# Symmetric attention: blocks of 1024 queries that meet whole blocks of keys, changed to halves of 512 that meet in a circle (72 units a pair of heads for 80)

## The chip, the core and the metric

The kernel runs on one core of one Trainium2 chip. Its engines have queues of their own: PE (TensorE) multiplies matrices, ACT (ScalarE) does the exponentials, DVE (VectorE) transposes and adds, POOL (GpSimd) copies small pieces, SP (SyncE) issues most transfers. The metric is the device time of one execution in microseconds (us); before the change it is 7413.25 us, the median of three runs (7411.64 to 7416.1).

## The reference, cut to what matters

Two layers work on an image batch of 4 x 128 channels x 64 x 64, so 4096 tokens an image. The first layer is a group norm, 1x1 convolutions and a channel-wide attention, the second an attention over 16 heads of 8 numbers, a feed-forward part and a recurrence. The change lies in the attention of the second layer. Query, key and value are the same array there, so the score matrix is symmetric:

```python
qkv = _qz_ring(heads + rx_theta)
q = jnp.transpose(qkv, (0, 2, 1, 3))
scores = jnp.einsum('bhsd,bhtd->bhst', q, q) / np.sqrt(D)
attn = jax.nn.softmax(scores, axis=-1)
ctx = jnp.einsum('bhst,bhtd->bhsd', attn, q)
```

The array that comes in is 4 x 4096 x 128. The denominators need no maximum taken off first, since the scores are bounded.

## The kernel before, in words

The images are worked on one after the other: a convolution stage (`first_stage`), then the attention (`second_stage`, which calls `attention`), and the feed-forward part of an image runs beside the convolution stage of the next. The last image's feed-forward part stands alone (`third_stage`), and the recurrence ends the program.

**Units.** `attention` loops over 8 pairs of heads. For each it cuts the 4096 tokens into 4 blocks (NQB) of 1024 queries and 32 tiles of 128 keys. A unit is one tile of keys against one block of queries, for both heads of the pair: 4 score matmuls (L839: two heads h, two halves x of 512 queries), 2 exponentials of 128x1024 on ACT (L848), and, two units later, `weigh` (L717), which multiplies the exponentials by the values and adds up in one PSUM bank `acc` for the whole block.

**Symmetry.** A block b meets its own 8 tiles (own units) and only the tiles of the blocks `behind` it in a circle: the next two blocks for b = 0 and 1, the next one for b = 2 and 3. `order` interleaves them. What the other blocks of queries would have needed is taken from the same exponentials, transposed. For an off-diagonal unit ACT also writes the sums over the queries (`accum_out`, an extra accumulator-read instruction on ACT) into `denom`; DVE transposes the two tiles of exponentials (`run_flips`, L684) into `flipped`, two more instructions; and PE multiplies them by `mirror` weights in `mirror_step` (L697). Four units make a group; a group takes 16 mirror steps of 8 matmul instructions, and after the last DVE adds the result into `later` (L708, L710).

**The order by hand.** PE, ACT, DVE and POOL follow program order in this stage. In each turn (one unit) come: scores, exponentials, `weigh` of the unit two turns back, as many mirror steps as a credit allows (`rates` is what a unit adds to it; at most 4.0 is kept), the steps that are due in `ends`, and up to two units' transposes (none in the first unit of a block). A group's steps may begin two turns after its fourth transposition was issued, and a group's first transposition waits until the group two before it is used up (`flipped` holds two groups).

**The end of a block.** `finish` runs when a block's last unit has been weighed, in the second unit of the next block: DVE transposes `acc` (o, L745), POOL copies it to `own` (L753, 16 copies). `mirrored` adds what other blocks left in `later` and `denom`: POOL copies the sums into order (L738), DVE transposes `later` (turned, L765), POOL copies (other, L772) and adds (L774, L775). `result` divides on DVE (L779, L780). For blocks 1 to 3 `mirrored` comes at once and `result` 6 turns later; block 0's wait for the next pair's block 0.

**Buffers.** `exps` (6) and parts of the image `xs` hold exponentials of five units; `ps_pair` (3 buffers of two PSUM banks) holds scores; `ps_acc` 1; `keys` 6 blocks; `turned` 2, shared by turned and other.

Of the kernel before, what the change touches and what calls it, by code (L numbers as in the profile page):

```python
# [26 lines left out]
def kernel(  # L27
# [32 lines left out]
    P = 128  # L60
# [498 lines left out]
    def attention(n, q, xs, tail, upcoming):  # L559
# [8 lines left out]

        qb = blocks(q)
        fixed, _ = here["fixed"]  # L570

        behind = [[(b + 1 + i) % NQB for i in range(2 if b < NQB // 2 else 1)] for b in range(NQB)]
        met_by = [[b for b in range(NQB) if k in behind[b]] for k in range(NQB)]
# [18 lines left out]
        def prepare(pair):  # L592
# [51 lines left out]
            later = get("later", f"later{n}_{pair}")  # L644
            denom = get("denom", f"denom{n}_{pair}")
# [44 lines left out]
        def mirror_step(state, s):  # L690
# [4 lines left out]
            for h in range(2):  # L695
                for x in range(2):
                    nc.tensor.matmul(  # L697
                        state["acc"][ts(2 * h + x, 32), :],
# [6 lines left out]
            if s == 15:  # L705
                dst = state["later"][:, ts(state["batch"], P)]
                if state["slot"] == 0:
                    nc.vector.tensor_copy(dst, state["acc"])  # L708
                else:
                    nc.vector.tensor_tensor(dst, dst, state["acc"], ALU.add)  # L710

        def weigh(it):
            if it["first"]:
                it["in"]["acc"] = get("ps_acc", "acc{}_{}_{}".format(n, *it["block"]))
            for h in range(2):
                for x in range(2):
                    nc.tensor.matmul(  # L717
                        it["in"]["acc"][ts(2 * h + x, 32), :],
                        it["qa"][:, ds((2 * it["jt"] + h) * V, 32)],
# [5 lines left out]

        def mirrored_sums(pair, b, denom):

            total = denom[:, 0, ts(b, QT), :]
            for slot in range(1, len(met_by[b])):
                by_key = small.tile([P, QT, 2], F32, tag="by_key", name=f"by_key{n}_{pair}_{b}")  # L730
                nc.gpsimd.tensor_tensor(by_key, total, denom[:, slot, ts(b, QT), :], ALU.add)
                total = by_key
# [8 lines left out]
        def finish(pair, b, block, later, denom):  # L741
# [5 lines left out]
            tag = "own" if b else "own_0"  # L747
# [9 lines left out]
            def mirrored():  # L757
# [6 lines left out]
                turned = get("turned", f"turned{n}_{pair}_{b}")  # L764
                nc.vector.transpose(turned, later[:, ts(b, 2 * P)])  # L765
                tv = turned.rearrange("p (y k a d) -> p k y a d", y=2, k=4, a=4)
                other = get("turned", f"other{n}_{pair}_{b}")[:, 0 : QT * 2 * D]
                to = other.rearrange("p (y a h d) -> p h y a d", y=2, a=4, h=2)
                for x in range(2):
                    for h in range(2):  # L770
                        for k in range(4):
                            nc.gpsimd.tensor_copy(to[ts(k, 32), h], tv[ts(2 * h + x, 32), k])  # L772
# [14 lines left out]
            if b:  # L787
                ends.append((turn, mirrored))
                ends.append((turn + 6, result))
            else:  # L790
                first.extend([mirrored, result])

        def order(b):

            own = list(range(QT * b, QT * (b + 1)))
            rest = [jt for k in behind[b] for jt in range(QT * k, QT * (k + 1))]
            each = len(rest) // QT
            return [
                jt for k in range(QT) for jt in rest[each * k : each * (k + 1)] + own[k : k + 1]
            ]  # L800

# [13 lines left out]
        ends, first = [], []  # L815
# [3 lines left out]
        for pair in range(NPAIR):  # L819
            keys, queries, qa, later, denom = ready  # L820
            for b in range(NQB):
# [7 lines left out]
                for at, jt in enumerate(tiles):  # L829
                    assert not (tail and jt // QT == NQB - 1)  # L830
                    name = f"{n}_{pair}_{b}_{jt}"
                    cols = ts(jt % QT, P)
                    off = jt // QT != b
                    slot = met_by[jt // QT].index(b) if off else None
                    ss = [pair_psum(f"s{name}_{h}") for h in range(2)]
                    for h in range(2):
                        for x in range(2):
# [3 lines left out]
                                keys[jt // QT].bitcast(F32R)[r, cols],  # L841
# [4 lines left out]
                    es = exps(name, end_of_all and at >= 2)  # L846
                    for h in range(2):
                        nc.scalar.activation(  # L848
                            es[h],
                            ss[h].rearrange("p x c -> p (x c)"),  # L850
# [82 lines left out]
        for _, end in ends[:-2]:  # L933
            end()
# [213 lines left out]
    def first_stage(im, before):  # L1148
# [11 lines left out]
        with stage(f"conv{n}", **pools, **psum), tc.manual_schedule(engines=engines):  # L1160
# [4 lines left out]
            def meanwhile(steps=1):  # L1165

                calls[0] += 1
                if before and calls[0] in (10, 11):
                    before["left"].pop(0)()
# [324 lines left out]
```

## Time and profile before

| | |
|---|---|
| runs | 7416.1, 7413.25, 7411.64 us; median 7413.25 |
| profiled execution | 7414.47 us, its span 7412.7 us, mean granted TensorE clock 0.984 |
| busy share of the span | PE 96%, ACT 82%, DVE 73%, PEld 46%, POOL 37% |
| attention stretches (434.6 to 1712.2, 2245.1 to 3522, 4054.2 to 5332, 5866.8 to 7145) | 1277.6, 1276.9, 1277.8, 1278.2 us |
| convolution stretches between them | 532.9, 532.2, 534.8 us |
| start to the first attention, and after the last | 434.6 and 267 us |

All times in the profile are us from the span's start unless marked ns. A group line names the line of the kernel, the engine, the operation, what is written and read, how often, then the busy time, the mean length of one instruction in ns and the engine's idle time before it. Instructions of PE, ACT and DVE overlap their neighbours a little, so the distance from start to start is shorter than the length. A busy PE need not be a PE at its peak.

### The profile page before, as it was taken

The numbers are of one execution on the slowest core, as the hardware profiler recorded it, in microseconds if no ns is written. First come the engines' busy times: TensorE is split into PE (matmuls) and PEld (weight loads), VectorE is DVE, ScalarE is ACT, GpSimd is POOL, SyncE is SP. The second block draws the span as 40 slices with busy tenths as digits, with TensorE's granted clock in tenths as the row PEclk, the third lists the DMA queues.
The fourth block names the chain that finished last, engine by engine and source line by source line (L and its number), as shares of the span: only waits on it lengthen the run. The fifth ranks groups of instructions, "written<-read, shape, count | busy, mean of one in ns | idle before, by whom it ended". The sixth has DMA issues, their size and how long they took to land. (4 is left out here: it accounts for less than half of the span.)

```text
span 7412.7 us, 212494 instructions
## 1 busy us (share of the span) xinstructions
PE 7153.2 (96%) x88078; PEld 3385.8 (46%) x88078; DVE 5395.9 (73%) x7364; ACT 6107.7 (82%) x9557; POOL 2730.3 (37%) x9769
## 2 busy tenths in 40 slices
PE   8999999999999999999899999999999999999977
PEld 3444444444444444444444444444444444444446
DVE  5677777776777777777677777777767777777764
ACT  3479999995448999999445999999844599999976
POOL 1034444343223434344323343444422243444342
PEclk9999999999999999999999999999999999999989
DMA  0010000000111000000011100000001100000012
GB/s 27 32 38 24 25 21 21 19 9 25 35 39 43 26 20 20 23 22 18 18 36 45 35 21 19 24 24 18 18 26 35 48 26 23 23 23 24 11 58 103
DMA packets 81537, 211.99 MB, mean 29 GB/s; under 512 B 8800, under 2 KB 8832, under 8 KB 79792
## 3 DMA queue, kind: packets, MB, share of 16 engines
q1 hardware_dynamic: 77312, 186.68, 7.4%
q8 instruction: 693, 11.35, 0.7%
q10 hardware_dynamic: 2016, 10.49, 0.3%
q14 instruction: 284, 2.33, 0.1%
q0 software_dynamic: 1232, 1.14, 0.1%
HBM read 141.65 MB, written 56.62 MB: 27 GB/s over the span
## 5 line engine op out<-in xcount | busy, mean ns | idle before, releaser
L848 ACT ACTIVATE e<-s 128x1024 f32<-128x1024 f32 x3144 | 3102.2, 1042 | 24.2 <-PE s L839 12.5
L684 DVE STREAM_TRANSPOSE t<-e 128x1024 f32<-128x1024 f32 x1896 | 2210.3, 1212 | 296.8 <-ACT e L848 296.7
L697 PEld LDWEIGHTS misc<-t,mirror 128*32 128x32 f32 x49152 | 1449.2, 110 | 1482.2 <-issue 1453.2
L848 ACT ACTIVATE xs<-s 128x1024 f32<-128x1024 f32 x1976 | 1960.5, 1040 | 13.3 <-PE s L839 2.3
L697 PE MATMUL misc<-t,mirror 128*32 128x128 f32 x49152 | 1801.0, 273 | 0.0
L717 PE MATMUL acc<-e,q_aug 128*32 128x512 f32 x12576 | 1682.6, 607 | 0.0
L684 DVE STREAM_TRANSPOSE t<-xs 128x1024 f32<-128x1024 f32 x1176 | 1372.6, 1211 | 195.7 <-ACT xs L848 195.7
L753 POOL COPY own<-o 32x36 f32<-32x36 f32 x2048 | 429.0, 209 | 2612.5 <-DVE o L745 2532.6
L839 PE MATMUL s<-queries,keys 32*128 32x512 f32 x10240 | 1372.8, 495 | 16.9 <-ACT e L848 15.5
L717 PE MATMUL acc<-xs,q_aug 128*32 128x512 f32 x7904 | 1053.3, 605 | 0.0
L407 PE MATMUL acc<-p,asmT 128*128 128x512 f32 x2048 | 982.9, 612 | 0.0
L392 ACT ACTIVATE p<-s 128x1024 f32<-128x1024 f32 x512 | 497.2, 1022 | 557.3 <-PE s L384 548.2
L839 PEld LDWEIGHTS s<-queries,keys 32*128 32x128 f32 x10240 | 535.4, 181 | 607.9 <-issue 279.5
L400 DVE TENSOR_TENSOR total<-total,p 128x1024 f32<-128x1024 f32 x448 | 575.0, 1284 | 298.2 <-ACT p L392 274.8
L654 POOL COPY mirror<-q 32x128 f32<-32x128 f32 x2048 | 604.2, 295 | 107.4 <-PE misc L697 19.7
L407 PEld LDWEIGHTS acc<-p,asmT 128*128 128x128 f32 x2048 | 360.7, 191 | 516.5 <-issue 514.3
L384 PE MATMUL s<-e,e 64*128 64x512 f32 x2048 | 521.8, 628 | 4.6 <-DVE asmT L301 4.3
L772 POOL COPY other<-turned 32x64 f32<-32x64 f32 x2048 | 474.0, 231 | 87.4
L717 PEld LDWEIGHTS acc<-e,q_aug 128*32 128x32 f32 x12576 | 250.2, 108 | 387.5 <-issue 379.0
L848 ACT ACTIVATION_READ_ACCUMULATOR e<-s 128x1 f32 x1896 | 418.7, 221 | 0.0
L384 PEld LDWEIGHTS s<-e,e 64*128 64x128 f32 x2048 | 179.7, 190 | 276.8 <-issue 263.4
L717 PEld LDWEIGHTS acc<-xs,q_aug 128*32 128x32 f32 x7904 | 156.3, 108 | 242.0 <-issue 226.3
(243 smaller groups left out, 4679.8 us busy)
## 6 DMA issues: line engine op xcount, KB each, us to landing
keys<-parts_dram SPq DMA_DIRECT2D x256, 256.0 KB
queries<-parts_dram SPq DMA_DIRECT2D x1024, 32.0 KB
fx<-x_dram SPq DMA_DIRECT2D x64, 256.0 KB
x_dram<-x SPq DMA_DIRECT2D x56, 256.0 KB
xs<-in_x_dram SPq DMA_DIRECT2D x16, 512.0 KB
t_dram<-t2T SPq DMA_DIRECT2D x32, 256.0 KB
t2s<-t_dram SPq DMA_DIRECT2D x16, 512.0 KB
parts_dram<-high SPq DMA_DIRECT2D x28, 256.0 KB
```

The lines of the kernel that those rows point to most:

```text
L384: nc.tensor.matmul(s[:, j, :], e2[rows, ts(2 * jp + j, P)], e1[rows, ts(ic, IC)], start=True, stop=True,)
L392: nc.scalar.activation(p, s, AF.Exp)
L400: nc.vector.tensor_tensor(state[ic], state[ic], p, ALU.add)
L407: nc.tensor.matmul(state["acc", ic], asmT[:, ts(2 * jp + j, P)], p[:, j, :], start=jp == 0 and j == 0, stop=jp == NP - 1 and j == 1,)
L654: nc.gpsimd.tensor_copy(wv[ts(a, 32), s, :, :, ts(a, D)], own[ts(s, 32)])
L684: nc.vector.transpose(group["e"][h][:, k, :], es[h])
L697: nc.tensor.matmul(state["acc"][ts(2 * h + x, 32), :], state["w"][:, QT * (s // 4) + TG * x + s % 4, h, :], state["e"][h][:, :, ds(IC * x ...
L717: nc.tensor.matmul(it["in"]["acc"][ts(2 * h + x, 32), :], it["qa"][:, ds((2 * it["jt"] + h) * V, 32)], it["e"][h][:, ts(x, IC)], start=it[ ...
L753: nc.gpsimd.tensor_copy(own[ts(s, 32), ts(x, 4), h, :], ov[ts(2 * h + x, 32), s, :, 0:V])
L772: nc.gpsimd.tensor_copy(to[ts(k, 32), h], tv[ts(2 * h + x, 32), k])
L839: nc.tensor.matmul(ss[h][:, x, :], keys[jt // QT].bitcast(F32R)[r, cols], queries[b].bitcast(F32R)[r, :], start=True, stop=True,)
L848: nc.scalar.activation(es[h], ss[h].rearrange("p x c -> p (x c)"), AF.Exp, scale=1.0 / math.sqrt(D), accum_out=denom[:, slot, jt, h : h + ...
```

## The change

The unit stays 128 keys against 1024 queries, but the two halves of the queries may now meet different tiles of keys. The eight half blocks of 512 stand in a circle; each meets itself and the next four halves (in blocks 0 and 1) or three (in blocks 2 and 3). An own unit pairs tile k of a block's first half with tile k of its second (4 units for 8). Most off-diagonal units use one tile for both halves, as before; four in each block are split, half x of the queries against tile `unit[x]`. A split unit has four exponentials of 512 columns, each with its own accumulator read, and its group is added into `later` in two halves. Blocks have 20, 20, 16 and 16 units for 24, 24, 16 and 16; of them 16, 16, 12 and 12 are off-diagonal, for 16, 16, 8 and 8.

With it: `denom` is laid out anew; `later` is cleared by POOL, and every group is added to it; `mirrored` and `result` of block 2 run in block 3, those of blocks 3, 0 and 1 in the next pair's block 0 (in its ninth, fourteenth and nineteenth unit, each `result` five turns later); after the last pair these three run at the end with scratch rooms of their own, and their results move into the next stage; the feed-forward part starts with block 2; the rates of the credit change; `turned` and `other` get a buffer each.

```diff
-        behind = [[(b + 1 + i) % NQB for i in range(2 if b < NQB // 2 else 1)] for b in range(NQB)]
-        met_by = [[b for b in range(NQB) if k in behind[b]] for k in range(NQB)]
+        met_by = [sorted((k - i) % NQB for i in range(3)) for k in range(NQB)]
...
+            nc.gpsimd.memset(later, 0.0)
...
-                        state["acc"][ts(2 * h + x, 32), :],
+                        state["acc"][ts(2 * x + h, 32), :],
...
-                dst = state["later"][:, ts(state["batch"], P)]
-                if state["slot"] == 0:
-                    nc.vector.tensor_copy(dst, state["acc"])
-                else:
-                    nc.vector.tensor_tensor(dst, dst, state["acc"], ALU.add)
+                whole = state["batch"][0] == state["batch"][1]
+                for x in range(1 if whole else 2):
+                    rows = slice(0, P) if whole else ts(x, P // 2)
+                    dst = state["later"][rows, ts(state["batch"][x], P)]
+                    nc.vector.tensor_tensor(dst, dst, state["acc"][rows, :], ALU.add)
...
-                        it["qa"][:, ds((2 * it["jt"] + h) * V, 32)],
+                        it["qa"][:, ds((2 * it["tiles"][x] + h) * V, 32)],
...
+        def third_sum(b):
+            return 2 * NT + (b - NQB // 2) * TG
...
+            total = small.tile([P, QT, 2], F32, tag="by_key", name=f"by_key{n}_{pair}_{b}")
+            nc.gpsimd.tensor_tensor(
+                total, denom[:, ts(b, QT), :], denom[:, ds(NT + b * QT, QT), :], ALU.add
+            )
+            if b >= NQB // 2:
+                odd = total[:, TG:QT, :]
+                nc.gpsimd.tensor_tensor(odd, odd, denom[:, ds(third_sum(b), TG), :], ALU.add)
...
-            if b:
-                ends.append((turn, mirrored))
-                ends.append((turn + 6, result))
-            else:
-                first.extend([mirrored, result])
+            if b == 2:
+                ends.append((turn + 8, mirrored))
+                ends.append((turn + 12, result))
+            elif b > 2:
+                late[0:0] = [mirrored, result]
+            else:
+                late.extend([mirrored, result])
...
-            own = list(range(QT * b, QT * (b + 1)))
-            rest = [jt for k in behind[b] for jt in range(QT * k, QT * (k + 1))]
-            each = len(rest) // QT
+            own = [(QT * b + k, QT * b + TG + k) for k in range(TG)]
+            halves = [(v, v) for v in range(2 * b + 2, 2 * b + (5 if b < NQB // 2 else 4))]
+            halves.insert(2, (2 * b + 1, 2 * b + (5 if b < NQB // 2 else 4)))
+            rest = [
+                tuple(v % (2 * NQB) * TG + k for v in vs) for vs in halves for k in range(TG)
+            ]
+            each = len(rest) // TG
+            return [u for k in range(TG) for u in rest[each * k : each * (k + 1)] + own[k : k + 1]]
...
+                    split = off and unit[0] != unit[1]
                     for h in range(2):
...
+                        for x in range(2 if split else 1):
+                            nc.scalar.activation(
+                                es[h][:, ts(x, IC)] if split else es[h],
+                                ss[h][:, x, :] if split else ss[h].rearrange("p x c -> p (x c)"),
+                                AF.Exp,
+                                scale=1.0 / math.sqrt(D),
+                                accum_out=denom[:, sums_at(b, unit[x]), h : h + 1] if off else None,
+                            )
-                    rates = (2.9, 2.2) if len(behind[b]) == 2 else (2.2, 1.9)
+                    rates = (3.3, 3.0) if b < NQB // 2 else (3.15, 3.0)
...
-                    if b == 0 and at == 10 and pair:
-                        ends.append((turn, first.pop(0)))
-                        ends.append((turn + 6, first.pop(0)))
+                    if b == 0 and pair and at in (7, 12, 17):
+                        ends.append((turn, late.pop(0)))
+                        ends.append((turn + 5, late.pop(0)))
...
-        first[0]()
-        ends.append((0, first[1]))
-        for _, end in ends[:-2]:
+        for _, end in ends:
             end()
-        return [end for _, end in ends[-2:]]
+        rooms = (None, half_tile(f"room0_{n}"), get("later", f"room1_{n}"))
+        for mirrored, room in zip(late[0::2], rooms):
+            mirrored(room)
+        return late[1::2]
...
-        order = [(i + NTG // NQB) % NTG for i in range(NTG)]
+        order = [(i + 2 * NTG // NQB) % NTG for i in range(NTG)]
...
-                if before and calls[0] in (10, 11):
+                if before and calls[0] in (10, 14, 18):
...
-            denom=((P, 2, NT, 2), 2),
-            later=((P, NT * 32), 2),
-            half=(HALF, 1),
-            turned=((P, 2 * P), 2),
+            denom=((P, 2 * NT + NQB // 2 * TG, 2), 2),
+            later=((P, NT * 32), 2),
+            half=(HALF, 1),
+            turned=((P, 2 * P), 1),
+            other=((P, QT * 2 * D), 1),
```

## The prediction, made before the changed kernel was run

> **What bounds the kernel now.** I read the 40 slices first: each image has an attention stretch where PE and ACT both stand at 9, and a convolution stretch where ACT stands at 4. I then cut one pair of heads (image 1, pair 6, whose units begin at 3044.2) into its four blocks of queries.
>
> ```profile
> core 0: us, PE busy (x) PEld busy (x) DVE busy (x) ACT busy (x) POOL busy (x), PEclk, DMA share, GB/s
> 3044.20:3092.60 48.40, 48.40 (x788) 23.19 (x784) 40.02 (x44) 48.16 (x82) 23.39 (x103) 1.00 0.07 26
> 3092.60:3141.00 48.40, 48.40 (x807) 23.38 (x800) 38.40 (x38) 48.14 (x81) 12.59 (x48) 1.00 0.03 8
> 3141.00:3171.50 30.50, 30.50 (x460) 13.82 (x456) 20.50 (x23) 30.49 (x49) 15.52 (x67) 1.00 0.09 28
> 3171.50:3202.60 31.10, 31.10 (x466) 14.04 (x458) 20.89 (x23) 30.98 (x50) 15.73 (x68) 1.00 0.10 32
> sum 158.40, PE 158.40 PEld 74.43 DVE 119.81 ACT 157.77 POOL 67.24; mean PE 39.60 PEld 18.61 DVE 29.95 ACT 39.44 POOL 16.81
> ```
>
> A pair takes 158.4 us, PE and ACT both look full, and shares cannot say which sets the pace. Starts can, so I read the timeline of PE inside the first block:
>
> ```profile
> 3050.34 0.51 PE L839 MATMUL s<-queries,keys 32*128 32x512 f32 x4
> 3050.78 1.07 PE L717 MATMUL acc<-e,q_aug 128*32 128x512 f32 x8
> 3051.66 0.84 PE L697 MATMUL misc<-t,mirror 128*32 128x128 f32 x24
> 3052.43 0.50 PE L839 MATMUL s<-queries,keys 32*128 32x512 f32 x4
> ...
> 3054.51 0.51 PE L839 MATMUL s<-queries,keys 32*128 32x512 f32 x4
> 3054.95 1.06 PE L717 MATMUL acc<-xs,q_aug 128*32 128x512 f32 x8
> 3055.84 0.62 PE L697 MATMUL misc<-t,mirror 128*32 128x128 f32 x16
> 3056.39 0.51 PE L839 MATMUL s<-queries,keys 32*128 32x512 f32 x4
> ```
>
> One unit runs from one L839 to the next. With 24 L697 matmuls (3 mirror steps of 8) it takes 2.09 us, with 16 (2 steps) 1.88; elsewhere in the block 2 steps give 1.87 and 4 give 2.31. So a unit costs PE 1.434 us plus 0.218 per step. Blocks 0 and 1 have 24 units each and 64 steps (four groups of 16): 24 x 1.434 + 64 x 0.218 = 48.4, exactly the window: PE sets the pace there. Blocks 2 and 3 give 16 x 1.434 + 32 x 0.218 = 29.9, but take 30.5 and 31.1. ACT says why:
>
> ```profile
> 3145.52 1.02 ACT L848 ACTIVATE e<-s 128x1024 f32<-128x1024 f32 x1
> 3146.44 0.19 ACT L848 ACTIVATION_READ_ACCUMULATOR e<-s 128x1 f32 x1
> 3146.53 1.02 ACT L848 ACTIVATE e<-s 128x1024 f32<-128x1024 f32 x1
> 3147.43 0.20 ACT L848 ACTIVATION_READ_ACCUMULATOR e<-s 128x1 f32 x1
> 3147.53 2.85 ACT L848 ACTIVATE e<-s 128x1024 f32<-128x1024 f32 x3
> ```
>
> Start to start an exponential with its accumulator read takes 1.00 us, one without 0.90 (about 0.10 being the read). An off-diagonal unit costs ACT 2.00, an own unit 1.80; 8 + 8 of them make 30.4, so ACT holds blocks 2 and 3, by 0.5 to 1.2 us each. The DVE lines are the third resource:
>
> ```profile
> L684 DVE STREAM_TRANSPOSE t<-e 128x1024 f32<-128x1024 f32 x1896 | 2210.3, 1212 | 296.8 <-ACT e L848 296.7
> L1004 ACT ACTIVATE hT<-ph,fb_sb 128x512 f32<-128x512 f32 x128 | 80.8, 683 | 62.8 <-PE ph L1001 62.6
> L294 ACT ACTIVATE ya<-pca,b_sb 128x1024 f32<-128x1024 f32 x16 | 17.9, 1119 | 64.1 <-PE pca L343 63.8
> DVE later L708 <- PE misc L697: 7.0, 6, 1.7
> DVE o L745 <- PE acc L717: 6.6, 4, 2.9
> DVE later L710 <- PE misc L697: 4.9, 3, 1.7
> DVE inv L779 <- POOL own L775: 4.5, 3, 1.7
> ```
>
> The last four are waits within that one pair. DVE is idle 158.4 - 119.8 = 38.6 us there.
>
> **The change, step by step.** Units per pair fall from 80 (24, 24, 16, 16) to 72 (20, 20, 16, 16). Own units fall from 32 to 16; off-diagonal ones rise from 48 to 56, groups from 12 to 14. Of the 56, 16 are split: two key tiles, so four 512-column exponentials with four reads.
>
> PE: blocks 0 and 1 become 20 x 1.434 + 64 x 0.218 = 42.6, blocks 2 and 3 16 x 1.434 + 48 x 0.218 = 33.4; the pair 152.1. The new credit rates feed this: 16 x 3.3 + 4 x 3.0 = 64.8 steps for 64, 12 x 3.15 + 4 x 3.0 = 49.8 for 48. Matmul shapes stay. Against 158.4: -6.3, of which 4.5 is PE work (156.6 to 152.1) and 1.8 is what ACT held back.
>
> ACT: no 512-column exponential is in the trace. Relu at 512 takes 683 ns (L1004) and at 1024 1119 (L294): 512 columns less save 436. So it starts 0.90 - 0.44 = 0.46 to 0.47 apart, and a split unit costs 4 x (0.47 + 0.10) = 2.26. The bound above: it keeps Relu's fixed part, 2 x 683 - 1119 = 247 ns against 1025 - 2 x 436 = 153 for the exponential, so 0.09 more each, 2.65 a unit; below, two halves cost one whole plus two reads, 2.2. I take 2.26, as the slope is per column and the fixed part is the exponential's own. Blocks 0 and 1: 4 x 1.80 + 12 x 2.00 + 4 x 2.26 = 40.2 under PE's 42.6; blocks 2 and 3: 7.2 + 16 + 9.0 = 32.2 under 33.4. ACT drops below PE everywhere.
>
> The Trainium skill speaks against the split ("ScalarE: Activation LUTs", What ACT_TABLE_LOAD costs): every ACTIVATE has a fixed part, about 186 ns with immediate scale and bias, plus 0.833 ns a column, and neighbours overlap by about 93. By it 512 columns would be 0.52 apart and a split unit an estimated 2.5; ACT would need 33.1 of 33.4 in blocks 2 and 3, and the sum would lose up to 1 us a pair. At 1024 columns the same rule gives 0.95 where this trace has 0.90.
>
> The split units come three or four in a row. ACT falls behind by 2.26 - 2.09 = 0.17 a unit, 0.5 to 0.7 after the row, and the three buffers of ps_pair, with two in use by a unit, forgive about 0.3 to 0.4: some 0.1 us lost a block.
>
> DVE: 8 more units, 16 more transposes. Four in a row take 4.58 us (3 starts and a last of 1.2), so 1.13 apart: +18.0 us a pair; split groups add into later in two halves, 14 groups making 18 adds for 12, at 0.21 apart: +1.3. Busy 119.8 becomes 139 of 152. Whether PE waits depends on when each group's fourth transposition ends. In a new block the first unit is not transposed before o, and o waits for the last weigh of the old block, 1.64 us into the second unit: 2.3 + 1.64 + 0.64 (o) + 8 x 1.13 = 13.6 us after the block's start. PE wants that group two turns later, in the seventh unit, after scores and weigh: 2 x 2.31 + 4 x 2.09 + 1.32 = 14.3. It fits by 0.7. The next three groups of block 0 end at 23.4, 34.0 and 44.6, late results and turned included, for needs at 24.9, 35.6 and 46.3. Block 1 has one result (0.45) before its first group: 0.2 is left. So no PE stall as drawn, with 0 to 1 us in blocks 0 and 1 as the bound (below nothing is excluded: PE has no work left out). I put 0.5 us on a pair for both engines' hitches: 152.6, -5.8, over 32 pairs -186.
>
> POOL: the memset of later (128x1024) is about 0.9 us by the 1.81 us row for twice its columns and runs where POOL is idle half the time. Three mirrored (9.3 us each on POOL's timeline, from by_key to the last own) now sit in block 0 with 4.0 of own copies and 5.3 of mirror weights: 37 of 42.6. DVE's result is queued 5 turns (10.7 us) behind its mirrored instead of 6, but the own copies no longer stand between; followed through, the tightest (block 0's) comes 0.5 us after POOL is done, so nothing. If POOL lags, the transposes behind it pay the 1.5 us each of L779. On SP the next pair's keys 2 and 3 and later queries queue for key buffers that block 3 reads until its fifteenth unit, before (keys 0) and after (keys 1, in split units) alike; they are needed some 20 us on, so nothing.
>
> Around the stage: pair 0 carries the tail of the convolution; its DVE work, some 12 us (8 rows of 0.69 us from arg to low, 22 of 0.2 to 0.36), no longer fits under PE: +2 us in each image, +8. The flush after the last unit has 3 or 4 steps more: +4. At three image borders DVE stood 7.4 us for other before the next image's q (it needed a turned buffer); the change gives it rooms, but POOL has a third mirrored in front of the feed-forward: -7.4 to +9 each, I take -3, so -9. At the end three mirrored instead of two stand before the last feed-forwards, whose DVE waited 13.1 us for POOL: +9.
>
> Sum: -186 + 8 + 4 - 9 + 9 = -174. The profiled execution took 7414.47 (span 7412.7, 1.8 around it), 1.2 above the median of 7413.25: 7240.5 there, 7240 as median.
>
> **Rivals.** *ACT takes the bound.* If a split unit costs 2.65, a row of four runs 1.7 us late in blocks 0 and 1 (44.3) and ACT needs 33.9 in the others: 156.4 a pair, -64 in all, 7350. For it: ACT already holds blocks 2 and 3. Against: copies of 512 columns (586 ns) lie near the smaller price.
>
> *DVE takes the bound (slower).* Its waits of today for later, o and inv (23.0 us a pair; 25 with 14 groups) stay as long as they are, because DVE is one queue in order and each wait pushes the transposes behind it. Then 139 + 25 = 164 a pair, +5.6, +180, 7590. It decides from 19 us of waits a pair on. For it: only 13 us of slack are left. Against: these waits are those of an engine that arrives early; when it runs behind, what it waits for is done.
>
> *The units fall but nothing follows*: PE's 1.434 could hold a share that belongs to ACT's pace. Then no gain, 7410. Against: it is 1.43 also in a unit without steps, where ACT would need more (7127.07 to 7128.50).
>
> **How the numbers follow.** The forecast 0.72, ACT 0.13, DVE 0.12, nothing 0.03. The forecast's own range: 2 us more a pair in hitches (+64) and +9 at each border (+36) give 7340; no hitches (-16), -7.4 at each border (-13) and nothing in pair 0 (-8) give 7203. To reach eight in ten it goes on to ACT's 7350: 7200 to 7350. This kernel's measurement can tell about 0.2% from no change. Faster by that: 0.72 + 0.13 = 0.85; within it 0.03; slower 0.12.
>
> **What would show it.** Windows of a pair near 42.8, 42.8, 33.5 and 33.5 us; ACT below 97% there; L684 with 3584 transposes, its waits on ACT mostly gone, DVE above 88%; a 512-column L848 near 590 ns. Wrong: "PEld misc" waiting for "DVE t" by tens of us (DVE), "PEld s" waiting for ACT in the split units (ACT), or 2.09 us units grown longer.

## The result, and the profile after

The changed kernel takes 7319.65 us (median of 4 runs, 7318.28 to 7323.84) against 7414.57 (4 runs, 7411.64 to 7416.1) for the kernel before on the same chips: ratio 0.9873, interval 0.9856 to 0.9891. That is 95 us less, where 174 were forecast. The profiled execution took 7318.31, its span 7316.6.

I begin with the windows of one pair, the same one as before (image 1, pair 6, whose units now begin at 3147.85), cut where each block's first scores start:

```profile
core 0: us, PE busy (x) PEld busy (x) DVE busy (x) ACT busy (x) POOL busy (x), PEclk, DMA share, GB/s
3147.85:3190.77 42.92, 42.92 (x758) 21.99 (x754) 39.66 (x46) 42.40 (x89) 24.84 (x111) 1.00 0.08 29
3190.77:3233.94 43.17, 43.07 (x756) 21.91 (x752) 39.55 (x42) 42.16 (x89) 20.31 (x80) 1.00 0.03 9
3233.94:3267.68 33.74, 33.74 (x582) 17.03 (x578) 29.34 (x30) 33.12 (x73) 7.94 (x32) 1.00 0.04 11
3267.68:3301.45 33.77, 33.77 (x581) 17.06 (x578) 29.35 (x32) 33.41 (x73) 15.92 (x69) 1.00 0.10 33
sum 153.60, PE 153.50 PEld 77.99 DVE 137.90 ACT 151.09 POOL 69.01; mean PE 38.38 PEld 19.50 DVE 34.48 ACT 37.77 POOL 17.25
```

The four windows were forecast at 42.8, 42.8, 33.5 and 33.5. DVE's busy time is 137.9 where 139 were worked out. The costliest groups of the page show the same from the other side:

```profile
PE 6989.7 (96%) x93198; PEld 3500.9 (48%) x93198; DVE 5984.1 (82%) x8068; ACT 5890.0 (81%) x11605; POOL 2772.9 (38%) x9929
...
L686 DVE STREAM_TRANSPOSE t<-e 128x1024 f32<-128x1024 f32 x2240 | 2586.3, 1207 | 6.3 <-ACT e L879 3.9
...
L686 DVE STREAM_TRANSPOSE t<-xs 128x1024 f32<-128x1024 f32 x1344 | 1558.2, 1207 | 2.2 <-ACT xs L879 0.8
```

2240 + 1344 = 3584 transpositions, as forecast, and DVE's idle time ahead of them, before the change nearly all of it spent waiting for ACT, has fallen from 296.8 (the group with e alone) to 6.3.

Then I cut the whole run at score starts, into attention (first to last unit of an image) and the gap from an image's last unit to the next image's first, or to the end of the span. These are my subtractions of start times in the two traces:

| us | before | after | difference | forecast |
|---|---|---|---|---|
| attention, images 0 to 3 | 1272.3, 1271.9, 1273.1, 1273.4 | 1232.2, 1235.7, 1234.5, 1235.5 | -152.8 | -178 (-186 + 8) |
| gaps at the three borders | 538.2, 537.2, 539.5 | 550.4, 559.7, 550.7 | +45.8 | -5 (flush +4, borders -9) |
| after the last unit | 272.1 | 283.2 | +11.1 | +9 |

So two terms missed: 25 us in attention, and 51 at the borders, the larger one by far. An ordinary border of after, by the timeline (start, length, engine, line, operation; in brackets the idle time before and its releaser). The last unit's scores started at 1666.95:

```profile
1683.13 0.60 DVE L713 TENSOR_TENSOR later<-later,misc 64x128 f32<-64x128 f32 x2 [4.63 <-PE misc L699]
1683.76 0.45 DVE L777 STREAM_TRANSPOSE turned<-later 128x256 f32<-128x256 f32 x1
1684.13 0.73 DVE L777 STREAM_TRANSPOSE room<-later 128x256 f32<-128x256 f32 x2
...
1689.18 0.44 POOL L789 TENSOR_TENSOR own<-own,other 128x128 f32<-128x128 f32 x1
1689.68 0.06 DVE L1191 MEMSET gap<- 128x1 f32 x1 [4.82 <-POOL own L789]
...
1689.83 3.74 DVE L331 TENSOR_SCALAR q<-xs,gm,r_g 128x512 f32<-128x512 f32 x8
...
1711.56 0.44 POOL L789 TENSOR_TENSOR own<-own,room 128x128 f32<-128x128 f32 x1
...
1712.03 0.69 DVE L990 TENSOR_TENSOR v<-pw,fx 128x512 f32<-128x512 f32 x1 [11.85 <-POOL own L789]
```

Before, the same instructions stood thus (last scores at 1707.3):

```profile
1716.81 0.06 DVE L1161 MEMSET gap<- 128x1 f32 x1
1717.60 1.92 DVE L331 TENSOR_SCALAR q<-xs,gm,r_g 128x512 f32<-128x512 f32 x4 [0.38 <-POOL r_g L228]
1726.90 0.45 DVE L765 STREAM_TRANSPOSE turned<-later 128x256 f32<-128x256 f32 x1 [7.39 <-POOL other L772]
1727.27 1.95 DVE L331 TENSOR_SCALAR q<-xs,gm,r_g 128x512 f32<-128x512 f32 x4
...
1731.53 0.68 DVE L960 TENSOR_TENSOR v<-pw,fx 128x512 f32<-128x512 f32 x1
```

The rooms did take away the 7.39 us wait for other. In its place DVE waits twice for POOL. First a tiny memset of the new stage (gap, it opens the stage's memory) starts 0.06 after POOL's first chain of copies and sums (one chain is the POOL part of one `mirrored`) has read other for the last time (1689.18 + 0.44); it holds q, which starts 22.9 us after the last scores for 10.3 before. Then v starts 0.03 after POOL's third chain has read its room (1711.56 + 0.44), at +45.1 for +24.3 before, and behind v in DVE's queue stand the e tiles that PE's convolutions need: the first convolution scores come at +68.4 for +56.3. From there to the stage's last accumulation (L407 before and after) it takes 479.1 to 481.2 us at the three borders of both kernels, so a border is longer by about as much as its first scores are late. At the second border, in the same view, the memset itself has to wait for the third chain:

```profile
3493.40 0.44 POOL L789 TENSOR_TENSOR own<-own,room 128x128 f32<-128x128 f32 x1
...
3493.90 0.06 DVE L1191 MEMSET gap<- 128x1 f32 x1 [23.80 <-POOL own L789]
```

That is the border that lost 22.5 us; the other two lost 12.1 and 11.2.

### The profile page after: what moved, and what is told of

It is laid out like the page before. It is cut to its first block, busy times and chain, and to the rows that moved or that the text cites. A ratio compares the mean times of both kernels' runs of the same rounds, so it can differ in the third digit from the quotient of the medians.

```text
span 7316.6 us, 225003 instructions
## 1 busy us (share of the span) xinstructions
PE 6989.7 (96%) x93198; PEld 3500.9 (48%) x93198; DVE 5984.1 (82%) x8068; ACT 5890.0 (81%) x11605; POOL 2772.9 (38%) x9929
## 3 DMA queue, kind: packets, MB, share of 16 engines
q0 software_dynamic: 1232, 1.14, 0.1%
## 5 line engine op out<-in xcount | busy, mean ns | idle before, releaser
L879 ACT ACTIVATE e<-s 128x1024 f32<-128x1024 f32 (+1 forms) x3480 | 2946.7, 889 | 59.1 <-PE s L867 35.9
L686 DVE STREAM_TRANSPOSE t<-e 128x1024 f32<-128x1024 f32 x2240 | 2586.3, 1207 | 6.3 <-ACT e L879 3.9
L699 PEld LDWEIGHTS misc<-t,mirror 128*32 128x32 f32 x57344 | 1665.3, 110 | 1403.7 <-issue 1348.6
L699 PE MATMUL misc<-t,mirror 128*32 128x128 f32 x57344 | 1998.7, 274 | 24.9 <-DVE later L713 17.4
L879 ACT ACTIVATE xs<-s 128x1024 f32<-128x1024 f32 (+1 forms) x2152 | 1834.9, 893 | 33.0 <-PE s L867 19.6
L686 DVE STREAM_TRANSPOSE t<-xs 128x1024 f32<-128x1024 f32 x1344 | 1558.2, 1207 | 2.2 <-ACT xs L879 0.8
L720 PE MATMUL acc<-e,q_aug 128*32 128x512 f32 x11360 | 1518.5, 606 | 0.0
L407 PE MATMUL acc<-p,asmT 128*128 128x512 f32 x2048 | 983.3, 612 | 0.0
L656 POOL COPY mirror<-q 32x128 f32<-32x128 f32 x2048 | 601.1, 293 | 239.0 <-PE misc L699 151.1
L879 ACT ACTIVATION_READ_ACCUMULATOR e<-s 128x1 f32 x2880 | 649.9, 226 | 0.0
L407 PEld LDWEIGHTS acc<-p,asmT 128*128 128x128 f32 x2048 | 361.5, 192 | 517.2 <-issue 515.0
L713 DVE TENSOR_TENSOR later<-later,misc 128x128 f32<-128x128 f32 (+1 forms) x576 | 162.5, 282 | 378.1 <-PE misc L699 373.7
L747 POOL COPY by_token<-by_key 32x4 f32<-32x4 f32 x2048 | 374.5, 183 | 86.4
```

The lines of the kernel that those rows point to most:

```text
L407: nc.tensor.matmul(state["acc", ic], asmT[:, ts(2 * jp + j, P)], p[:, j, :], start=jp == 0 and j == 0, stop=jp == NP - 1 and j == 1,)
L656: nc.gpsimd.tensor_copy(wv[ts(a, 32), s, :, :, ts(a, D)], own[ts(s, 32)])
L686: nc.vector.transpose(group["e"][h][:, k, :], es[h])
L699: nc.tensor.matmul(state["acc"][ts(2 * x + h, 32), :], state["w"][:, QT * (s // 4) + TG * x + s % 4, h, :], state["e"][h][:, :, ds(IC * x ...
L720: nc.tensor.matmul(it["in"]["acc"][ts(2 * h + x, 32), :], it["qa"][:, ds((2 * it["tiles"][x] + h) * V, 32)], it["e"][h][:, ts(x, IC)], sta ...
L879: nc.scalar.activation(es[h][:, ts(x, IC)] if split else es[h], ss[h][:, x, :] if split else ss[h].rearrange("p x c -> p (x c)"), AF.Exp, ...
```

## The experiments

Times are of the profiled run, unless an interval is given; after is 7318.3 there. The kernel before took 7409 to 7412 us (medians) beside these runs for 7414.57 beside the result, so a difference of some 5 us in the total tells nothing by itself; the lengths of gaps and blocks in the traces tell more. "+12.9" means us after the last unit's scores of an image.

**e1: the memset on another engine.**

```diff
-            nc.vector.memset(get("gap", f"gap{n}")[:, 0:1], 0.0)
+            nc.gpsimd.memset(get("gap", f"gap{n}")[:, 0:1], 0.0)
```

> The memset of the tile gap, the first thing of the convolution stage, is issued by POOL and not by DVE. Theory M (memory that POOL's three late mirrored steps still read holds DVE at the image borders): after the change DVE stood 4.82, 23.80 and about 4.8 us at this memset; without that q begins some 18 us after the last unit at all three borders (22.9, 41.0 and 23.0 us measured), the second border gets 10 to 20 us shorter than its 559.7, the first and third (550.3 and 550.7) change by less than 5, since there DVE still waits at v (11.85 us) for the same POOL chain. In all -10 to -25 us. Theory F (the flush of the last block, later by DVE's load, sets the border, and the memset's wait only lies beside it): every border stays within 3 us.

7313.9. The q starts at +12.9 at all three borders (+22.9, +41.0 and +23.0 in after). But the gaps are 550.9, 552.1 and 554.4: only the second gains, 7.6, less than the 10 to 20 expected. What is late next at the first and third border is v, as e1's timeline shows at the first:

```profile
1679.14 3.74 DVE L331 TENSOR_SCALAR q<-xs,gm,r_g 128x512 f32<-128x512 f32 x8 [1.35 <-POOL r_g L228]
...
1710.82 0.23 POOL L790 TENSOR_TENSOR own<-own,by_token 128x16 f32<-128x16 f32 x1
1710.90 0.69 DVE L990 TENSOR_TENSOR v<-pw,fx 128x512 f32<-128x512 f32 x1 [20.43 <-POOL own L789]
```

The wait for POOL grew from 11.85 to 20.43 and v is where it was. At the second border v lies elsewhere in memory and does not wait (+23.2), and still the first convolution scores come only at +70.4. There DVE waits one step further on, as the DVE and then the POOL timeline of that border show (its last scores started at 3453.3):

```profile
3504.83 1.12 DVE L255 TENSOR_SCALAR v<-v,mv_v,r_v 128x128 f32<-128x128 f32 x4 [21.10 <-POOL r_v L228]
...
3503.77 1.02 POOL L228 TENSOR_TENSOR r_v<-v_v,minus_half 128x4 f32<-128x4 f32 x1
```

The small r_v, which DVE needs to normalise v, stands in POOL's own queue behind the third chain, which ends at 3501.4, and three memsets. So the chain holds DVE in two ways: through the memory it still reads, and through POOL's order. Half of the theory stands: the memset held q, and q was not what set the border.

**e2: one chain on POOL at an image's end for three.**

```diff
-        for mirrored, room in zip(late[0::2], rooms):
+        for mirrored, room in zip(late[0:2:2], rooms):
```

> Left out: after the last pair of each image the mirrored steps of blocks 0 and 1 (only block 3's runs), so the results of these two blocks lack what other blocks computed for them. Theory M: two of three POOL chains of 9.3 us are gone, DVE's waits at gap and v with them: the borders fall from 550.3, 559.7 and 550.7 us to about 543 each, and the end after the last unit (283.2 us) by 9 to 18; in all -35 to -50 us. Theory F: the borders keep what the flush costs and fall by less than 3 us each; only the end gains.

7261.7. Gaps 537.0, 542.9, 540.2 and 265.6 at the end: 13.4, 16.8, 10.5 and 17.5 less than after, 58 in all. That is more than the 35 to 50 expected. The last addition into later still comes at +15.7 to +16.7 and q at +22.4 to +23.1, so the flush stayed as late as in after: what came back is the price of the two further chains on POOL (9.3 us each). What the late flush costs beside them this run does not tell, since the kernel before had two chains there and this one has one.

**e3: one exponential for a split unit, as in the others.**

```diff
-                    split = off and unit[0] != unit[1]
+                    split = False
+            nc.gpsimd.memset(denom, 1.0)
```

> Left out: a split unit is exponentiated as a whole (one ACTIVATE of 1024 columns a head, one accumulator read), so the sums of its second tile are missing and those of the first are wrong. Theory S (ACT falls behind in the row of split units): the own unit behind the row, 2.31 us on PE for 2.09 expected, falls to 2.09, and the last split unit by 0.02 to 0.05; about -1.0 us a pair, -33 us in all. Rival P (PE or DVE are held by the two key tiles or by the adds in two halves): the 2.31 stays, less than 5 us in all.

7284.1. A pair takes 152.2 in images 0 and 2 and 152.4 in 1 and 3, for 153.4 and 153.6; the PE model said 152.1. The own unit behind a row of split units takes 2.09 for 2.31, in all four blocks. Only the seventh unit of block 1 stays long (2.39). The split costs 1.18 us a pair, and the four attention stretches together are 35.7 shorter; the PE model is right to 0.3 a pair.

**e4: the kernel before without accumulator reads in blocks 2 and 3.**

```diff
-    accum_out=denom[:, slot, jt, h : h + 1] if off else None,
+    accum_out=denom[:, slot, jt, h : h + 1] if off and b < 2 else None,
```

> The kernel before, with the accumulator reads of blocks 2 and 3 left out (their sums are missing from the denominators). Theory A (ACT set the pace of blocks 2 and 3 before the change, PE that of blocks 0 and 1): blocks 2 and 3 fall from 30.5 and 31.0 us to 29.9 each, blocks 0 and 1 stay at 48.4; -1.5 to -1.8 us a pair, -45 to -58 us in all. Rival: these two blocks were held by something else (DVE's order, PE itself), under -15 us.

7389.7. Blocks 48.27, 48.33, 30.50 and 30.41 for 48.44, 48.35, 30.58 and 30.97: 0.8 a pair where 1.4 to 1.8 were expected. With 1.6 us less work for ACT, block 2 gains 0.08. So the sum "8 x 2.00 + 8 x 1.80" was not the pace of the block. What remains is local. In e4's timeline two units are clearly longer than the PE model, each behind a unit with 0 or 1 mirror step. In block 2 one of 3 steps takes 2.45 for 2.09: DVE's inv waits for POOL, so DVE comes late to its copy into later, and PE's mirror steps start 0.14 after that copy ends. In block 3 one of 4 steps takes 2.54 for 2.31: its scores wait for ACT, since the unit ahead, without a step, takes PE 1.44 where ACT needs 1.8. The two places, in e4's timeline (PEld is PE's weight load):

```profile
3304.73 0.25 DVE L780 RECIPROCAL inv<-own 128x16 f32<-128x16 f32 x1 [2.02 <-POOL own L776]
3305.31 0.28 DVE L709 COPY later<-misc 128x128 f32<-128x128 f32 x1
3305.73 0.86 PE L698 MATMUL misc<-t,mirror 128*32 128x128 f32 x24
...
3334.39 0.43 PEld L840 LDWEIGHTS s<-queries,keys 32*128 32x128 f32 x4 [0.84 <-ACT e L849]
```

No run takes away either of these two waits by itself.

**e5: q and the convolutions let go early, and the feed-forward part begun from the ninth call of `meanwhile`** (with the memset on POOL as in e1, and the sums of blocks 3 and 0 put into order before o).

```diff
                 for _ in range(steps):
                     step_first(own)
-                step_late()
+                if calls[0] > 8:
+                    step_late()
```

> The changed kernel with its attention as it is and three edits at the image border: the memset of gap on POOL; the sums of blocks 3 and 0 copied on POOL before o instead of behind it (POOL stood idle 8.9 us there); the feed-forward of the previous image begins after the eighth call of meanwhile (end of the two projections) and not at the first, so that DVE does not come to v before POOL's chain is done. Theory M (POOL's chain of three mirrored steps, through reused memory and POOL's own queue, holds DVE): q begins some 13 us after the last unit for 22.9, 41.0 and 23.0; no wait of over 3 us at v; the first scores of the convolution stage come before 55 us (68.4, 77.7, 68.5 now); the borders fall from 550.3, 559.7 and 550.7 to 530 to 542; in all -30 to -60 us. Theory F (the later flush sets it): -10 us at most.

7315.1: a miss. The first convolution scores come at +52.0, +48.4 and +51.4, as the theory wanted, but the gaps are 554.5, 550.9 and 553.3. From these scores to the stage's last accumulation it now takes 496 to 498 us for 481, and behind it another 3.7 to 6.5 for 1.0: the last feed-forward step (wx_stats), begun later at the same spacing, ends at +542 to +547 for +522 to +532. So the 16 to 29 us won at the start were given back, most of them inside the stage. A likely reason, not tried by itself, is that the feed-forward's work, which used to run partly ahead of the convolutions, now runs beside them.

**e6: all three results of the pair before 3 turns later.**

```diff
-                        ends.append((turn + 5, late.pop(0)))
+                        ends.append((turn + 8, late.pop(0)))
+                        ends.sort(key=lambda e: e[0])
```

> The results of blocks 3, 0 and 1 come eight turns behind their mirrored steps instead of five. Theory D (DVE's slack before a block's first group is under 0.5 us, and block 1's extra reciprocal and multiply overdraw it): the seventh unit of block 1, 2.40 us for 2.09, falls to 2.09, block 1 from 43.13 to 42.85, -8 us in all. Rival: the 0.31 is of another cause (the weights mirror, POOL) and stays: within 2 us.

7326.9: a miss; block 1 takes 43.24 for 43.17 in this pair (43.39 for 43.13 in images 0 and 2), its seventh unit 2.46. In the timeline the second result now stands where the third had been, ahead of block 1's first group; the experiment did not do what it was made for. e12 moves the third result alone.

**e7: own units placed elsewhere** (after 4, 8, 10 and 16 off-diagonal units in blocks 0 and 1; 3, 6, 10 and 12 in 2 and 3), so that at most two split units follow each other.

```diff
-            each = len(rest) // TG
-            return [u for k in range(TG) for u in rest[each * k : each * (k + 1)] + own[k : k + 1]]
+            at = (4, 8, 10, 16) if b < NQB // 2 else (3, 6, 10, 12)
...
```

> The own units stand elsewhere: in blocks 0 and 1 the third own unit comes after the second split unit (two rows of two for one of four), in blocks 2 and 3 the third own unit between the second and third. Theory S (ACT lags 0.2 us for each split unit in a row and the own unit behind pays): the 2.31 of these own units falls towards 2.1, -0.5 to -0.9 us a pair, -16 to -29 us in all. But by the credit arithmetic the first transposes of most groups are then put off by one unit, as the group two before is not used up. Theory D (DVE has under 1 us of slack a group): PE then waits for transposes, 0.2 to 1 us a group, +1 to +8 us a pair, and the kernel gets slower by 30 to 250 us.

7305.5. Blocks 42.69, 42.64, 33.77 and 33.83 (images 0 and 2) for 42.87, 43.13, 33.67 and 33.73: -0.47 a pair, just short of the 0.5 to 0.9 expected, and 10 over the four attention stretches. Blocks 0 and 1 gain, 2 and 3 lose 0.1 each, and the DVE stall of the other theory does not come; that of block 1's seventh unit (2.08 here) is gone too, so not all of the gain is ACT's.

**e8 and e9: what was learned at the borders, alone and with the order of e7.** The memset on POOL; the feed-forward from the ninth call and every 14 calls for 15; in the last image POOL's sums earlier and the copies out of the rooms on ACT. In e9 the own units also stand at (4, 8, 10, 16) and (3, 6, 9, 12), the latter being the changed kernel's own order.

```diff
-            step_late = in_steps(feed_forwards(before) if before else [], 15, 2)
+            step_late = in_steps(feed_forwards(before) if before else [], 14, 2)
...
-                            nc.gpsimd.tensor_copy(to[ts(k, 32), h], tv[ts(2 * x + h, 32), k])
+                            copy = nc.scalar.copy if room is not None and n == N - 1 else nc.gpsimd.tensor_copy
+                            copy(to[ts(k, 32), h], tv[ts(2 * x + h, 32), k])
```

> The same without the moved own units: attention as in the changed kernel (153.4 to 153.6 us a pair); borders and end as in the run of all edits; 7260 to 7300.

> All edits meant to help together: gap's memset on POOL, the feed-forward from the ninth call of meanwhile and a new one every 14 calls for 15 (before it, begun late with 15, the last one ended 30 us later and ran on alone), for the last image alone the sums of blocks 3 and 0 before o and the copies of the two rooms on ACT, and in blocks 0 and 1 the own unit between the split ones (blocks 2 and 3: between third and fourth). Theory M with the total of work in mind: borders 538 to 548 us for 550 to 560, end 268 to 276 for 283, pair 152.8 to 153.1 for 153.4 to 153.6; 7250 to 7285 us, 0.980 to 0.983 of the kernel before. Theory F (border fixed by the later flush and by the work of the stage): border within 3 us of 550; 7290 to 7305.

e8: 7299.3; gaps 554.0, 542.1, 554.7, end 272.7. e9: 7290.65 (5 runs), ratio to before 0.9837, 0.9824 to 0.9851, above the 7250 to 7285 expected. The last stretch is back at the 272 of before; two of three borders are still at 552 to 555, and there v waits until +50 for POOL's third chain. From the first convolution scores to the last accumulation it takes 496 to 500, as in e5.

**e10: one transposition more in the third unit of blocks 0 and 1.**

```diff
+                    if at == 2 and b < NQB // 2 and not flips:
+                        nc.vector.transpose(groups[-1]["e"][0][:, 2, :], es[0])
```

> The changed kernel with one transposition more (1.13 us of DVE) in the third unit of blocks 0 and 1, the same data written twice. Theory D (DVE's slack before a block's first group is 0 to 0.7 us, as worked out): PE waits 0.4 to 1.1 us in block 0's seventh unit and about 1.1 more in block 1's; blocks 42.9 to 43.3-44.0 and 43.1 to 44.2; +1.5 to +2.2 us a pair, +48 to +70 in all. Rival (DVE has several us of slack, and block 1's 0.31 is of another cause): under +10 us.

7387.4, +69. Block 0 takes 43.99 for 42.87, block 1 44.27 for 43.13: +1.12 and +1.14, as much as a transposition takes from start to start (1.13). DVE, at 92% in these blocks, has nothing to spare ahead of a block's first group. Each 1.13 us more there costs a whole 1.13 us, twice a pair.

**e11: as e9, the feed-forward from the thirteenth call.**

```diff
-                if calls[0] > 8:
+                if calls[0] > 12:
```

> The run of all edits with the feed-forward from the thirteenth call of meanwhile for the ninth. At the first and third border DVE still stood about 8 us at v (until 49.8 and 50.6 us after the last unit), where v lies on a room that POOL reads; at the second, where it lies elsewhere, the border was 543.7 for 552.3 and 553.3. Theory M: by the thirteenth call POOL is done, the first and third border fall to 543 to 547, the second stays within 3 us; -10 to -18 us, 7273 to 7281. Theory W (the work of the stage has a fixed sum, a later feed-forward only ends later): within 4 us of 7290.

7278.05 (5 runs, 7276.0 to 7279.29) against 7411.86 (9 runs), ratio 0.9819, 0.9806 to 0.9833. Gaps 542.0, 544.0, 544.5, end 272.9; first convolution scores at +44.4, +45.2 and +45.5. The first border, in e9 (its DVE and PE lines, last scores at 1666.3) and below the dots in e11 (last scores at 1666.7):

```profile
1716.11 0.69 DVE L997 TENSOR_TENSOR v<-pw,fx 128x512 f32<-128x512 f32 x1 [7.93 <-POOL own L791]
1719.40 2.08 PE L384 MATMUL s<-e,e 64*128 64x512 f32 x4 [7.34 <-DVE asmT L301]
...
1711.04 1.13 PE L384 MATMUL s<-e,e 64*128 64x512 f32 x4
1717.97 0.68 DVE L997 TENSOR_TENSOR v<-pw,fx 128x512 f32<-128x512 f32 x1
```

With v behind the convolutions' first steps in DVE's queue, it no longer waits for POOL or holds them: the first and third gap are 10.3 and 8.8 shorter than in e9. (The first pair of image 2 takes 4.3 more, for a reason that was not looked for.) This version beats both kernels: 134 us under before, and some 40 under after by the two ratios to before. The borders are still 3.8 to 6.8 us longer than before: their first convolution scores come 10 to 14 earlier, but from there to the last accumulation it takes 497 to 498.

**e12: the last result alone moved past block 1's first group.**

```diff
-                        ends.append((turn + 5, late.pop(0)))
+                        ends.append((turn + (5 if at < 17 else 12), late.pop(0)))
```

> One part of the changed kernel is moved: the last of the three results of the pair before (block 1's) is queued 12 turns after its sums for 5, so that none of the three stands in the first seven units of block 1. (In e6 all three went 3 turns later, and the second of them came to stand where the third had been.) Theory G: PE's first mirror steps of a new group wait for DVE's add of the group before, which stands in DVE's queue behind the new group's eight transpositions; in block 1 a result of 0.45 us stands there too. In the trace of after the add ends at 3205.18 and the steps begin at 3205.32, 0.31 late. Without the result the add ends 0.45 earlier: 0.14 is left over, the seventh unit of block 1 takes 2.08 to 2.10 for 2.39, block 1 42.85 to 42.90 for 43.17, the pair 153.3; 0.28 x 32 = -9, a profiled time of 7307 to 7313. The seventh unit of block 0 stays at 2.09 with nothing to spare. Rival: the place of the result does not matter (as e6 seemed to say), because the engine that holds the steps is another one: the seventh unit stays at 2.39 and the time at 7317 to 7322.

7311.4. The stall is in the timeline of after, at the start of block 1 (first scores at 3190.77), first DVE's lines and below the dots PE's:

```profile
3194.64 0.72 DVE L754 STREAM_TRANSPOSE o<-acc 128x512 f32<-128x512 f32 x1 [0.84 <-PE acc L720]
3195.39 2.37 DVE L686 STREAM_TRANSPOSE t<-e 128x1024 f32<-128x1024 f32 x2
3197.68 4.58 DVE L686 STREAM_TRANSPOSE t<-xs 128x1024 f32<-128x1024 f32 x4
3202.19 0.21 DVE L794 RECIPROCAL inv<-own 128x16 f32<-128x16 f32 x1
3202.43 0.29 DVE L795 TENSOR_TENSOR q<-own,inv 128x128 f32<-128x128 f32 x1
3202.64 2.37 DVE L686 STREAM_TRANSPOSE t<-e 128x1024 f32<-128x1024 f32 x2
3204.93 0.25 DVE L713 TENSOR_TENSOR later<-later,misc 128x128 f32<-128x128 f32 x1
...
3203.51 0.29 PE L699 MATMUL misc<-t,mirror 128*32 128x128 f32 x4
3203.73 0.50 PE L867 MATMUL s<-queries,keys 32*128 32x512 f32 x4
...
3205.32 0.86 PE L699 MATMUL misc<-t,mirror 128*32 128x128 f32 x24
```

DVE does not stop once from o to the addition: eight transpositions, a result, the addition of the group before. That group's last mirror step on PE was over at 3203.80, but its addition is queued behind the transpositions. PE's steps of the new group start 0.14 after it ends, 1.59 after their unit's scores where 1.32 is usual. In e12's timeline, DVE and then PE, the result is gone from this place:

```profile
3200.61 2.33 DVE L686 STREAM_TRANSPOSE t<-e 128x1024 f32<-128x1024 f32 x2
3202.86 0.25 DVE L713 TENSOR_TENSOR later<-later,misc 128x128 f32<-128x128 f32 x1
...
3202.14 0.50 PE L867 MATMUL s<-queries,keys 32*128 32x512 f32 x4
...
3203.45 0.82 PE L699 MATMUL misc<-t,mirror 128*32 128x128 f32 x21
```

The steps begin 1.31 after their scores, the seventh unit takes 2.08 and block 1 42.86 for 43.17: -0.3 a pair, 7.6 over the four attention stretches, and the whole run is 7 us shorter.

## Why the prediction was right, and where it was wrong

**Right.** The direction, and the price of the main part. "16 x 1.434 + 48 x 0.218" and its sister made 152.1 a pair; e3, where of the hitches only block 1's 0.31 is left, measures 152.2 to 152.4. ACT fell back: a split unit was priced at 2.26 and takes 4 x 0.57 = 2.28, as this row of after shows, which settles the rival with 2.65 (ACT's timeline in a row of four split units, the columns as before):

```profile
3170.84 0.20 ACT L879 ACTIVATION_READ_ACCUMULATOR e<-s 128x1 f32 x1
3170.93 0.60 ACT L879 ACTIVATE e<-s 128x512 f32<-128x512 f32 x1
3171.41 0.21 ACT L879 ACTIVATION_READ_ACCUMULATOR e<-s 128x1 f32 x1
3171.50 0.61 ACT L879 ACTIVATE e<-s 128x512 f32<-128x512 f32 x1
...
3178.24 0.31 ACT L879 ACTIVATION_READ_ACCUMULATOR e<-s 128x1 f32 x1
3178.33 0.71 ACT L879 ACTIVATE e<-s 128x512 f32<-128x512 f32 x1
```

From one ACTIVATE to the next (3170.93 to 3171.50) is 0.57, and the read begins 0.48 after its ACTIVATE. The fixed part of the Trainium skill ("ScalarE: Activation LUTs", What ACT_TABLE_LOAD costs) gave an estimated 0.52 apart without the read; the slope of this kernel's own rows was nearer, and the measurement decides. DVE as a whole did not become the bound. Its waits for later, o and inv did not fade as the prediction argued, except those for inv; in the same pair of after they are

```profile
DVE later L713 <- PE misc L699: 11.2, 12, 1.6
DVE o L754 <- PE acc L720: 4.1, 4, 1.2
```

and none for inv: 15.3 us for 23.0, under the 19 from which the second rival decides. They fill what DVE has to spare (137.9 of work and 15.3 of waits in 153.6), the pair stays near PE's sum, and the rival's 164 did not come. Pair 0 costs 4.4 us more in all (block 0 there against later pairs: 31.4 before, 35.8 after) for 8 forecast, and the end 11.1 for 9.

**Wrong, the borders: "-7.4 to +9 each, I take -3".** They cost 12.1, 22.5 and 11.2, all outside the bounds. The step counted POOL's third chain as work in front of the feed-forward, and looked at which waits of the old stage would go. It did not ask who in the next stage takes over the memory that the chain still reads (the memset, which stands before q, and v, which stands before e), nor what stands behind the chain in POOL's queue (r_v). e1 shows the memset's hold on q, e2 that two chains cost 10 to 17 us a border, and e11 against e9 that v's place in the queue costs 9 to 10 at two of them. DVE itself also comes later out of the image: PE stood 4.35 us for its statistics (gmv) where it stood 1.16 before, and the last addition into later is at +16.5 for +9.2, where the flush was priced at one us an image. What that alone costs stays open: with that flush still late, e2's gaps are 540.0 on average against 538.3 before, but e2 has one chain less than before.

**Wrong, the hitches: "0.5 us on a pair".** Against the PE model they are 1.3 to 1.5. The first part is ACT's: "some 0.1 us lost a block" is 0.25 to 0.34 (most of it an own unit behind a row of split ones, 0.22 longer), 1.18 over the four blocks, and e3 takes it away. The second is 0.31 in block 1. The walk through DVE's queue was right to 0.2 as far as it went: with block 0's 13.6 and one result of 0.45 the eighth transposition should end 14.1 after the block's start, and it ends at 14.2. What the walk forgot is the addition of the group before (0.25 in one piece, 0.56 in two halves), which stands behind the transpositions and has to be done, with 0.14 from its end to PE, before PE may write misc again. With these the 0.7 of slack in block 0 is 0.0 and the 0.2 in block 1 is -0.2; e10 finds nothing left in either and e12 takes the stall away.

**Wrong in size and place: "1.8 is what ACT held back".** By e4, ACT's accumulator reads held back 0.8, most of it in block 3 and hardly any in block 2, so the sum over a block was not the limit; what was left there sits behind the units with few mirror steps, in block 2 as a wait for DVE and POOL. The gain came all the same: in e3 blocks 2 and 3 take 33.39, the 33.4 of the PE model. After the change most units have 3 steps.

By these steps: 0.89 a pair too little, 28, less 3.6 in pair 0, is the 25 missed in attention; with 51 at the borders and 2 at the end that is the 78 between -174 and -96, the difference of the two profiled runs. That the total still lies inside the stated range is partly luck: its upper end allowed 36 more at the borders, which took 51, and 64 more for hitches, which took 28.

## What to carry to other kernels

Price the edges of a stage as carefully as its steady state: for each buffer that a change keeps busy longer, ask which instruction of the next stage writes that memory first, and what stands behind it in its queue; and for each engine whose queue grows, ask which small result of the next stage has to wait behind that. An engine at 90% over a stretch can have nothing to spare at one point of it, so walk its queue to that point with every small instruction in, those that free an accumulator above all. When work is put off, look at where it then ends.

## What was not expected of the hardware

ACT's recorded lengths grew through a row of 512-column exponentials from 0.60 to 0.71 us, and its reads from 0.20 to 0.31, while starts stayed 0.57 apart; ACT's busy share of the pair was still 98% (151.1 of 153.6; "below 97%" was forecast), where the distances from start to start add up to an estimated 145.3 (16 x 1.80 + 40 x 2.00 + 16 x 2.28), 95%. Only these distances gave its pace. And on this path nothing was absorbed: 1.13 us more on DVE in one place of a block made the block 1.12 and 1.14 longer.
